# Local attention in a decoder: the second product with the values stationary, probabilities divided ahead of their flip, a norm's bias folded into a weight

## The chip, the cores and the metric

The kernel runs on one core of one Trainium2 chip. The metric is the device time of one execution in microseconds, as the median of several runs; lower is better. The core has TensorE (PE, whose loads of the stationary operand are shown apart as PEld), VectorE (DVE), ScalarE (ACT), GpSimd (POOL) and SyncE (SP), which issues the DMAs. [...]

## The reference

One decoder layer on x of shape (2, 512, 128): a Mamba block with a mixture of experts, cross-attention to a context of 32 rows, and a stack of six layers of local attention and FFN, each of the three followed by a LayerNorm without weights. The change lies in the six-layer stack. With `shift_tokens` (the second half of the channels taken from the token before), 16 heads of 64 and windows of 32 tokens, it is, cut:

```python
def local_attention(q, k, v):            # (b, h, n, d), w = 32
    bq, bk, bv = (t.reshape(b, h, nw, w, d) for t in (q, k, v))
    bk2, bv2 = look(bk), look(bv)        # window before, then own window: 64 keys
    sim = jnp.einsum('bhwie,bhwje->bhwij', bq, bk2) * QK_SCALE
    sim = jnp.where(mask, -jnp.finfo(sim.dtype).max, sim)
    attn = jax.nn.softmax(sim, -1)
    return jnp.einsum('bhwij,bhwje->bhwie', attn, bv2).reshape(b, h, n, d)

def attn_layer(x, Wqkv, qs, ksc, Wo):
    q, k, v = heads of x @ Wqkv
    q, k = l2norm(q) * qs, l2norm(k) * ksc      # then rotary, with a scale by position
    return merge(local_attention(q, k, v)) @ Wo

def ffn_layer(x, g, bln, W1, b1, W2, b2):
    xn = (x - mu) / jnp.sqrt(var + 1e-05) * g + bln
    a, gate = jnp.split(xn @ W1 + b1, 2, -1)
    return a * jax.nn.gelu(gate, approximate=False) @ W2 + b2

for i in range(6):
    x = attn_layer(shift_tokens(x), ...) + x
    x = ffn_layer(shift_tokens(x), ...) + x
```

All arithmetic of the stack is in f32.

## The kernel before

**The front** (Mamba, experts, cross-attention) runs up to about 453 us and is not touched. Then comes the local stack, from line 600 on.

**Layout.** z holds x with channels on partitions, two batches of 512 tokens (plus two columns for the shift). A unit of work is a tile: 128 tokens of one batch in one layer, 6 x 2 x 4 = 48 tiles. Each is an object `Tile` with methods, called at three successive steps of one loop over s: at step s, tile s is A (project, square, rotate, values, sums, norm), tile s-1 is B (flips of q and k, scores, softmax), tile s-2 is C (flip of the probabilities, second product, division, output). An `Ffn` is made when the fourth tile of a batch has been C; it is F1 in the step after (mean, variance, spread) and F2 in the one after that (hidden, out). The loop is inside a block that keeps every engine's queue in program order, so the order of the calls in one step is the order of the queues:

```python
B_.keys_before(); A.begin(); A.project(0); A.square(0); A.rotate(0)
C.flip_p(); F1.mean(); A.project(1); A.square(1); A.rotate(1)
B_.flip_q(); C.attend(); C.weigh(); B_.flip_k(); F2.hidden()
B_.scores(); B_.softmax(); C.flip_o(); B_.expo(); F1.var(); F2.out()
A.values(); A.sums(0); A.sums(1); C.out(); F1.spread(); A.norm(); F1.table()
```

**What each does.** `project` (L712) makes q or k of 128 tokens and 16 heads in a PSUM tile `qk_ps` of 128 x 1024. `square` (L717, ACT) and `rotate` (L724 and L728 on DVE, the sum L733 on POOL) read it. `sums` (L737, DVE) reduces the squares by head. `norm` takes the inverse root: ACT L755, L679 and L680, then POOL L756 and L681 to L684, then POOL multiplies q and k by it (L759, two instructions). `flip_q` and `flip_k` (L892) turn these by eight transposes each, in two groups of four, and ACT copies each group out of PSUM (L893). `scores` puts the mask (L786) and 64 small products (L797) in the PSUM tile `sim`; row 32j + q of it is a query of one window and one head, its columns are four head groups, two slots and 64 keys. `softmax` (L808, L810, DVE) subtracts the row's maximum, `expo` (L814, ACT) takes the exponential.

`flip_p` turns the exponentials (eight transposes of s, L892) into pT, with keys on partitions. `attend` (L833) multiplies: 64 products, each a block of pT (64 keys x 32 queries) as the stationary operand and 65 columns of values as the moving one, of which the last is one, so that column 64 of the result is the sum of the probabilities. The values lie in va (own windows) and vb (shifted by 32 rows, by a DMA from va), both filled with ones at the start (L664). The result, in two PSUM tiles `av`, has queries on partitions. `weigh` (L847, L848, DVE) divides by column 64; `flip_o` (L863) turns the result by eight transposes, which ACT copies to oT (L865, L867); `out` (L882), for two tiles at once and so in every second step, multiplies with Wo, and DVE adds the residual (L885).

**PSUM.** Tag a has three buffers of two banks, for qk_ps (twice a step), av (twice), sim and v_ps. Tag b has two buffers of one bank, for all else.

**FFN.** `mean` subtracts the mean and squares; `var` makes the inverse root; `spread` (L938, DVE) multiplies by it and by ln_g, and POOL adds ln_b (L939); `hidden` multiplies with W1 in three chunks for each half, Gelu on ACT with b1 as bias (L953), and DVE adds b1 of the other half and multiplies (L954); `out` (L963, L966) is the second product.

## Time and profile before

| | |
|---|---|
| time, median of 3 runs | 1481.08 us (1478.0 to 1482.82) |
| the profiled execution's own time | 1485.97 us |
| its span | 1484.2 us |
| PE, DVE, ACT, POOL busy | 1237.8, 908.5, 631.0, 699.6 us |
| granted TensorE clock, mean | 0.912 |
| local stack, first projection to the end | 454.9 to 1484.2 us |
| waits of POOL L756 for ACT L755 (norm) | 294.8 us |
| waits of DVE L724 for ACT L717 | 126.0 us |
| waits of PE's transposes for POOL L759 | 50.9 us |
| waits of POOL L939 for DVE L938 | 27.6 us |

The page gives the busy time of each engine over the whole span, the chain of work that ended last, and the costliest groups of instructions with the idle time ahead of them and what ended it. PE records are pipelined: a matmul's record is longer than its share of the array's time, so distances from start to start say more than durations. Stretches of one step each (from the first qk_ps of a step to that of the next) show what differs between the steps.

### The profile page before, as it was taken

What the parts mean: (1) busy time and instruction counts of PE and PEld (TensorE: products, weight loads), DVE (VectorE), ACT (ScalarE), POOL (GpSimd) and SP (SyncE); (2) the same over time, 40 slices, a digit from 0 to 9 for tenths busy, and PEclk for the clock granted to TensorE, in tenths of its full rate; (3) what the DMA queues carried; (4) which work ended last, traced back from release to release, by engine and by line L of the source; (5) the groups of instructions that cost most, each with busy time, mean ns of one, the idle gap of its engine ahead of it and who ended that gap; (6) DMA issues with size and microseconds to landing.
All of it is one profiled execution on the core that took longest, in us unless ns stands there. A gap on an engine that the chain in (4) does not pass through costs nothing.

```text
span 1484.2 us, 37129 instructions
## 1 busy us (share of the span) xinstructions
PE 1237.8 (83%) x16523; PEld 755.4 (51%) x16523; DVE 908.5 (61%) x1085; ACT 631.0 (43%) x1044; POOL 699.6 (47%) x705
## 2 busy tenths in 40 slices
PE   6686899989646888888898899989888989898865
PEld 2223355545323555655566565656565655555553
DVE  3687866665445665656666565766575666556522
ACT  3333332222113545555555455555555555445521
POOL 1468773100206664564645554647456554455410
PEclk9668999999857999999999999999999999999966
DMA  8122220000300110211121112111021110001000
GB/s 287 59 64 83 78 66 0 30 1 1 131 18 15 42 35 17 70 45 45 31 62 54 30 31 68 47 41 34 17 70 45 42 31 27 27 16 31 27 2 14
DMA packets 39691, 68.04 MB, mean 46 GB/s; under 512 B 4878, under 2 KB 20748, under 8 KB 39532
## 3 DMA queue, kind: packets, MB, share of 16 engines
q1 hardware_dynamic: 39532, 65.68, 14.7%
q8 instruction: 130, 2.13, 0.6%
q14 instruction: 29, 0.24, 0.0%
HBM read 41.00 MB, written 0.70 MB: 28 GB/s over the span
## 4 chain that ended last, share of the span: by engine, by line
PE 52%; DVE 16%; POOL 9%; issue 7%; ACT 7%; POOLq 0%; ACTq 0%; DVEq 0%
PE t_ps L892 6%; PE sim L797 5%; PE wo_ps L882 5%; PE d_ps L403 4%; POOL t L759 4%; PE qk_ps L712 4%; PE av L833 3%; PE v_ps L745 3%; PE g_ps L416 3%; PE u_ps L417 3%; PE fa_ps L951 2%; DVE t L728 2%; PE fg_ps L949 2%; PE fo_ps L963 2%; PE t_ps L863 2%
## 5 line engine op out<-in xcount | busy, mean ns | idle before, releaser
L733 POOL TENSOR_TENSOR t<-t,t 128x1024 f32<-128x1024 f32 x96 | 225.2, 2359 | 30.9 <-DVE rd L847 26.1
L724 DVE TENSOR_TENSOR t<-qk_ps,tab 128x1024 f32<-128x1024 f32 x96 | 117.4, 1223 | 126.0 <-ACT sq L717 126.0
L712 PE MATMUL qk_ps<-wqkv,z 128*128 128x512 f32 x384 | 182.5, 599 | 1.8 <-POOL z L659 1.6
L759 POOL TENSOR_TENSOR t<-t,rn 128x1024 f32<-128x1024 f32 x96 | 180.6, 1903 | 3.8
L892 PE MATMUL t_ps<-ident,t 128*128 128x128 f32 x768 | 115.5, 299 | 51.2 <-POOL t L759 50.9
L756 POOL TENSOR_SCALAR ss<-ss 128x32 f32<-128x32 f32 x48 | 13.7, 286 | 295.8 <-ACT sc L755 294.8
L892 PEld LDWEIGHTS t_ps<-ident,t 128*128 128x128 f32 x768 | 93.9, 153 | 89.6 <-POOL t L759 72.1
L717 ACT ACTIVATE sq<-qk_ps 128x1024 f32<-128x1024 f32 x96 | 98.1, 1023 | 77.8 <-PE qk_ps L712 67.2
L728 DVE TENSOR_TENSOR t<-qk_ps,tab 128x1024 f32<-128x1024 f32 x96 | 116.5, 1213 | 0.0
L737 DVE TENSOR_REDUCE ss<-sq 128x16 f32<-128x1024 f32 x96 | 112.2, 1209 | 0.3
L808 DVE TENSOR_REDUCE m<-sim 128x16 f32<-128x1024 f32 x48 | 58.8, 1224 | 76.4 <-PE sim L797 76.4
L712 PEld LDWEIGHTS qk_ps<-wqkv,z 128*128 128x128 f32 x384 | 70.3, 193 | 64.7 <-issue 60.6
L745 PE MATMUL v_ps<-wqkv,z 128*128 128x512 f32 x192 | 98.8, 640 | 0.0
L278 ACT ACTIVATE da<-dl,acol 128x512 f32<-128x512 f32 x64 | 44.2, 691 | 126.4 <-DVE hs L307 90.1
L295 PE MATMUL y<-hs,ident 128*128 128x512 f32 x128 | 78.3, 746 | 20.2 <-POOL hs L313 12.1
L285 POOL TENSOR_TENSOR db<-dx,b_sb 128x1024 f32<-128x1024 f32 x32 | 76.3, 2390 | 39.5 <-DVE dx L257 22.8
L797 PE MATMUL sim<-kT,qT 64*32 64x64 f32 x6144 | 78.1, 229 | 18.7 <-issue 18.5
L797 PEld LDWEIGHTS sim<-kT,qT 64*32 64x32 f32 x6144 | 66.6, 107 | 43.0 <-issue 41.7
L882 PE MATMUL wo_ps<-oT,wo 128*128 128x256 f32 x384 | 88.2, 383 | 0.0
L893 ACT COPY kT<-t_ps 128x512 f32<-128x512 f32 x96 | 52.6, 588 | 76.0 <-PE t_ps L892 75.8
L882 PEld LDWEIGHTS wo_ps<-oT,wo 128*128 128x128 f32 x384 | 73.8, 193 | 20.3 <-issue 10.8
L833 PE MATMUL av<-va,pT 64*32 64x65 f32 x3072 | 80.9, 248 | 3.5 <-issue 3.2
(232 smaller groups left out, 2411.8 us busy)
## 6 DMA issues: line engine op xcount, KB each, us to landing
vb<-va SPq DMA_DIRECT2D x48, 390.0 KB, 3.6
wqkv<-in_L_ffn_Wqkv_dram SPq DMA_DIRECT2D x18, 512.0 KB, 5.9
b_sb<-bcd SPq DMA_DIRECT2D x32, 256.0 KB, 3.2
c_sb<-bcd SPq DMA_DIRECT2D x21, 256.0 KB, 3.1
vb<-va SPq DMA_DIRECT2D x36, 130.0 KB, 3.4
wo<-in_L_ffn_Wo_dram SPq DMA_DIRECT2D x6, 512.0 KB, 4.3
wg<-in_L_attn_Wg_dram SPq DMA_DIRECT2D x8, 256.0 KB, 6.1
wu<-in_L_attn_Wu_dram SPq DMA_DIRECT2D x8, 256.0 KB, 5.5
```

The lines of the kernel that those rows point to most:

```text
L712: mm(pa[:, hf * S : (hf + 1) * S], self.xb, w[:, w0 : w0 + S], start=True, stop=True)
L717: nc.scalar.activation(sq.rearrange("p h d -> p (h d)"), self.raw[qk], AF.Square)
L724: nc.vector.tensor_mul(t1, pa.rearrange("p (h d) -> p h d", d=DH), tab[:, 2 * qk, ti, :].unsqueeze(1).to_broadcast([P, H, DH]),)
L728: nc.vector.tensor_mul(t2.rearrange("p h (x d) -> p h x d", x=2), swap_halves(pa), tab[:, 2 * qk + 1, ti, :].rearrange("p (x d) -> p x d", ...
L733: nc.gpsimd.tensor_add(t1, t1, t2)
L737: nc.vector.tensor_reduce(self.ss[:, qk], self.sq[qk], AX.X, ALU.add)
L745: mm(pv[:, hf * S : (hf + 1) * S], self.xb, w[:, w0 : w0 + S], start=True, stop=True)
L759: nc.gpsimd.tensor_mul(self.rot[qk], self.rot[qk], self.rn[:, qk].unsqueeze(2).to_broadcast([P, H, DH]),)
L797: mm(ps[32 * j : 32 * j + 32, par, hg, slot, :], qT[64 * r : 64 * r + 64, 2 * hg + c, WIN * w : WIN * (w + 1)], kT[64 * r : 64 * r + 64, 2 ...
L833: mm(po[hh][32 * at : 32 * at + 32, g, i * DV : (i + 1) * DV], pT[rows, 4 * par + hg, 32 * j : 32 * j + 32], (self.v if par else self.v2)[ ...
L882: mm(po, wo_l[:, c, :], self.oT[:, c, :], start=c == 0, stop=c == INNER // P - 1)
L892: tr(pt[:, n, :], src[:, (4 * g + n) * P : (4 * g + n + 1) * P], ident)
```

## The change

Three edits, all in the local stack.

1. **Division ahead of the flip.** `weigh` now belongs to B, after the sums of A: DVE reduces the exponentials over the 64 keys and takes the reciprocal, and POOL multiplies the exponentials by it, in place. The column of ones goes; va and vb have 64 columns, and only the first 32 rows of vb are set to zero at the start.
2. **Values stationary.** `attend` takes 64 columns of values as the stationary operand and 32 columns of pT as the moving one. The result, one PSUM tile, has the channels on partitions and queries along the row, as `out` needs it: two ACT copies (one for each slot) go straight to oT. `flip_o` is gone.
3. **Bias through W1.** `fold_bias` multiplies ln_b with W1 once for each layer, by six one-column products, and DVE adds b1; `hidden` takes this as its bias, and POOL's add in `spread` goes. It is called at the start of the step in which A is tile 2 of batch 0.

```diff
-    va = [big.tile([P, H, DV], F32, name=f"va{j}") for j in range(4)]
-    vb = [big.tile([P, H, DV], F32, name=f"vb{j}") for j in range(3)]
-    for v in va + vb:
-        nc.gpsimd.memset(v, 1.0)
+    va = [big.tile([P, H, DH], F32, name=f"va{j}") for j in range(4)]
+    vb = [big.tile([P, H, DH], F32, name=f"vb{j}") for j in range(3)]
+    for v in vb:
+        nc.gpsimd.memset(v[0:WIN], 0.0)
...
+        def weigh(self):
+            s = self.sf.rearrange("p (x k) -> p x k", k=64)
+            rd = tmp.tile([P, 16], F32, tag="rd", name="rd")
+            nc.vector.tensor_reduce(rd, s, AX.X, ALU.add)
+            nc.vector.reciprocal(rd, rd)
+            nc.gpsimd.tensor_mul(s, s, rd.unsqueeze(2).to_broadcast([P, 16, 64]))
...
         def attend(self):
-            po = [psa.tile([P, 2, S], F32, tag="a", name=f"av{hh}") for hh in range(2)]
-            for g in range(2):
-                for c in range(2):
-                    for r in range(2):
-                        for hh in range(2):
-                            for w in range(4):
-                                slot, par = divmod(w, 2)
-                                hg, j, i = 2 * hh + g, 2 * c + (r ^ par), 2 * c + r
-                                rows, at = slice(64 * slot, 64 * slot + 64), (w + 2 * hh) % 4
-                                mm(
-                                    po[hh][32 * at : 32 * at + 32, g, i * DV : (i + 1) * DV],
-                                    pT[rows, 4 * par + hg, 32 * j : 32 * j + 32],
-                                    (self.v if par else self.v2)[rows, 4 * hg + i, :],
-                                    start=True, stop=True,
-                                )
+            po = psa.tile([P, 2, H // 2, 2, WIN], F32, tag="a", name="av")
+            for hg in range(4):
+                for c in range(2):
+                    for par in range(2):
+                        for slot in range(2):
+                            for r in range(2):
+                                j, i = 2 * c + (r ^ par), 2 * c + r
+                                rows = slice(64 * slot, 64 * slot + 64)
+                                mm(
+                                    po[64 * r : 64 * r + 64, slot, 2 * hg + c, par, :],
+                                    (self.v if par else self.v2)[rows, 4 * hg + i, :],
+                                    pT[rows, 4 * par + hg, 32 * j : 32 * j + 32],
+                                    start=True, stop=True,
+                                )
+            for slot in range(2):
+                t0 = (self.ti % 2) * P + 64 * slot
+                nc.scalar.copy(
+                    self.oT[:, :, t0 : t0 + 64], po[:, slot].rearrange("p c a q -> p c (a q)")
+                )
...
+    def fold_bias(layer, i):
+        w1, pf = layer[2], psb.tile([P, 6], F32, tag="b", name="b1_ps")
+        b1 = lw.tile([P, 6], F32, tag="b1", name=f"b1_{i}")
+        for k in range(6):
+            g, (f0, fs) = k // 3, FCH[k % 3]
+            w0 = g * DFF + f0
+            mm(pf[0:fs, k : k + 1], w1[:, w0 : w0 + fs], col(C_LNB + i), start=True, stop=True)
+            nc.vector.tensor_add(b1[0:fs, k : k + 1], pf[0:fs, k : k + 1], col(C_B1 + 6 * i + k, fs))
+        layer.append(b1)
...
             nc.vector.scalar_tensor_tensor(xc, xc, col(C_LNG + i), spread(self.rs), ALU.mult, ALU.mult)
-            nc.gpsimd.tensor_scalar_add(xc, xc, col(C_LNB + i))
...
+                if (b, ti) == (0, 2):
+                    fold_bias(layers[i], i)
...
             if C:
                 C.attend()
-                C.weigh()
...
                 B_.softmax()
-            if C:
-                C.flip_o()
             if B_:
                 B_.expo()
...
                 A.sums(0)
                 A.sums(1)
+            if B_:
+                B_.weigh()
             if C:
                 C.out()
```

More of the change, by code (lines that the diff above doesn't have):

```diff
@@ L627, in load_layer @@
         tab = lw.tile([P, 4, 4, DH], F32, tag="tab", name=f"tab_{i}")
-        return wqkv, wo, w1, w2, tab, qs
+        return [wqkv, wo, w1, w2, tab, qs]
     def scale_tables(layer):
-        tab, qs = layer[4:]
+        tab, qs = layer[4:6]
         nc.gpsimd.tensor_mul(tab, rot, qs.unsqueeze(2).to_broadcast([P, 4, 4, DH]))
@@ L649, in decoder_kernel @@
     NTB = S // P
-    DV = DH + 1
     z = big.tile([P, B, S + 2], F32, name="z")
@@ L746, in values @@
             v = self.v = va[n % 4]
-            nc.scalar.copy(v[:, :, 0:DH], pv.rearrange("p (h d) -> p h d", d=DH))
+            nc.scalar.copy(v.rearrange("p h d -> p (h d)"), pv)
             v2 = self.v2 = vb[n % 3]
@@ L820, in attend @@
         def attend(self):
-            pT = self.pT
-            po = [psa.tile([P, 2, S], F32, tag="a", name=f"av{hh}") for hh in range(2)]
-            for g in range(2):
-                for c in range(2):
-                    for r in range(2):
-                        for hh in range(2):
-                            for w in range(4):
-                                slot, par = divmod(w, 2)
-                                hg, j, i = 2 * hh + g, 2 * c + (r ^ par), 2 * c + r
-                                rows, at = slice(64 * slot, 64 * slot + 64), (w + 2 * hh) % 4
-                                mm(
-                                    po[hh][32 * at : 32 * at + 32, g, i * DV : (i + 1) * DV],
-                                    pT[rows, 4 * par + hg, 32 * j : 32 * j + 32],
-                                    (self.v if par else self.v2)[rows, 4 * hg + i, :],
-                                    start=True, stop=True,
-                                )
-            self.po = po
-        def weigh(self):
-            po = self.po
-            o = self.o = tmp.tile([P, H, DH], F32, tag="o", name="o", bufs=1)
-            for hh in range(2):
-                pe = po[hh][:, :, 0 : 4 * DV].rearrange("p g (i e) -> p g i e", e=DV)
-                rd = tmp.tile([P, 2, 4], F32, tag="rd", name="rd")
-                nc.vector.reciprocal(rd, pe[:, :, :, DH])
-                nc.vector.tensor_mul(
-                    o[:, 8 * hh : 8 * hh + 8, :].rearrange("p (g i) d -> p g i d", g=2),
-                    pe[:, :, :, 0:DH], rd.unsqueeze(3).to_broadcast([P, 2, 4, DH]),
-                )
-        def flip_o(self):
             if self.ti % 2:
@@ L857, in flip_o @@
                 self.oT = tmp.tile([P, H // 2, 2 * P], F32, tag="oT", name="oT")
-            dst = self.oT[:, :, (self.ti % 2) * P : (self.ti % 2 + 1) * P]
-            of = self.o.rearrange("p h d -> p (h d)")
-            for g in range(2):
-                pt = psb.tile([P, 4, P], F32, tag="b", name="t_ps")
-                for n in range(4):
-                    tr(pt[:, n, :], of[:, (4 * g + n) * P : (4 * g + n + 1) * P], ident)
-                if g == 0:
-                    nc.scalar.copy(dst[:, 0:4, :], pt)
-                else:
-                    nc.scalar.copy(
-                        dst[:, 4:8, :].rearrange("p c (x t) -> p c x t", x=2),
-                        bass.AP(
-                            tensor=pt.tensor, offset=pt.offset + 64,
-                            ap=[list(pt.ap[0]), [P, 4], [-64, 2], [1, 64]],
-                        ),
-                    )
+            pT = self.pT
+            po = psa.tile([P, 2, H // 2, 2, WIN], F32, tag="a", name="av")
[17 more added lines that the diff above has]
+                )
         def out(self):
@@ L921, in spread @@
         return sd
+    def fold_bias(layer, i):
[7 more added lines that the diff above has]
+        layer.append(b1)
     class Ffn:
         def __init__(self, i, b, layer):
-            self.i, self.b, (self.w1, self.w2) = i, b, layer[2:4]
+            self.i, self.b, (self.w1, self.w2), self.b1 = i, b, layer[2:4], layer[6]
         def mean(self):
@@ L952, in hidden @@
                 ge = ftmp.tile([P, S], F32, tag="ge", name="ge", bufs=2)
-                nc.scalar.activation(ge[0:fs], pg[0:fs], AF.Gelu, bias=col(C_B1 + 6 * i + 3 + c, fs))
+                nc.scalar.activation(ge[0:fs], pg[0:fs], AF.Gelu, bias=self.b1[0:fs, 3 + c : 4 + c])
                 nc.vector.scalar_tensor_tensor(
-                    hid[0:fs, c, :], pa[0:fs], col(C_B1 + 6 * i + c, fs), ge[0:fs], ALU.add, ALU.mult
+                    hid[0:fs, c, :], pa[0:fs], self.b1[0:fs, c : c + 1], ge[0:fs], ALU.add, ALU.mult
                 )
```

## The prediction

> **What bounds the kernel now.** I read the page first: engines, then the chain of work that ended last.

> ```profile
> PE 1237.8 (83%) x16523; PEld 755.4 (51%) x16523; DVE 908.5 (61%) x1085; ACT 631.0 (43%) x1044; POOL 699.6 (47%) x705
> PE 52%; DVE 16%; POOL 9%; issue 7%; ACT 7%; POOLq 0%; ACTq 0%; DVEq 0%
> ```

> TensorE is busy for 83% but holds only 52% of the chain: it is not the only limit. The change lies in the local stack, 48 steps from 454.9 us (first qk_ps of step 0) on. The step repeats in rounds of four, told apart by what C and the FFN add: R1 (C is tile 2: nothing), R2 (tile 3: wo_ps), R3 (tile 0, and F1), R4 (tile 1: wo_ps, and F2). Second, the busy times of four stretches, one round (layer 3, first batch), cut where each step's first qk_ps starts:

> ```profile
> 922.89:935.91 13.02, 12.74 (x303) 8.69 (x302) 9.66 (x13) 6.16 (x11) 9.81 (x9) 1.00 0.34 107
> 935.91:955.21 19.30, 17.21 (x320) 12.45 (x319) 13.21 (x14) 11.73 (x20) 10.35 (x12) 0.91 0.12 36
> 955.21:974.08 18.87, 16.08 (x322) 10.72 (x321) 12.45 (x15) 10.36 (x20) 10.45 (x13) 1.00 0.19 54
> 974.08:1001.27 27.19, 24.99 (x338) 14.25 (x337) 15.70 (x18) 13.52 (x20) 11.85 (x12) 1.00 0.18 51
> ```

> The columns are stretch, length, busy us of PE, PEld, DVE, ACT, POOL, the clock, DMA. R1 is all PE; R2 to R4 have 2 to 3 us each in which PE waits. For what, the timeline of each engine tells. In R2, on POOL and then PE:

> ```profile
> 938.55 0.28 POOL L756 TENSOR_SCALAR ss<-ss 128x32 f32<-128x32 f32 x1 [5.23 <-ACT sc L755]
> ...
> 940.52 3.76 POOL L759 TENSOR_TENSOR t<-t,rn 128x1024 f32<-128x1024 f32 x2
> ```
> ```profile
> 935.91 1.88 PE L712 MATMUL qk_ps<-wqkv,z 128*128 128x512 f32 x4
> 937.63 1.04 PE L892 MATMUL t_ps<-ident,s 128*128 128x128 f32 x8
> 938.50 1.88 PE L712 MATMUL qk_ps<-wqkv,z 128*128 128x512 f32 x4
> ```

> PE has done both projections by 940.4 and then waits to 942.5 for the norm's first product. This loop bounds R2: flip_q, scores, softmax, sums (both on DVE), norm (ACT, then POOL), flip_q. The sums end at 938.10, 4.77 us after the scores end; the first L759 ends 4.32 later. In R4 the same wait is 1.86 us, there because the bias stands in POOL's queue ahead of the norm:

> ```profile
> 975.13 1.58 POOL L939 TENSOR_SCALAR ln_xc<-ln_xc,cols 128x512 f32<-128x512 f32 x1 [2.10 <-DVE ln_xc L938]
> 976.78 0.29 POOL L756 TENSOR_SCALAR ss<-ss 128x32 f32<-128x32 f32 x1
> ...
> 978.45 3.77 POOL L759 TENSOR_TENSOR t<-t,rn 128x1024 f32<-128x1024 f32 x2
> ```

> In R3 PE waits 1.28 us at ln_sd for the variance's chain through softmax, exponential, ACT and POOL.

> [...] eight 128-column loads of ln_var take 0.97 us, 111 ns from one to the next. [...] the 128 records of L833 (64 products, two records each) take 1.49 us, their loads 1.33, some 10 ns each[...]. [...] after R2's wait L833 took 2.07 us at clock 0.50, with no wait 1.49:

> ```profile
> 943.50:945.70 2.20, 2.07 (x128) 1.83 (x128) 0.50 0.04 7
> 962.30:963.90 1.60, 1.49 (x128) 1.33 (x128) 1.00 0.00 0
> ```

> [...] Here 1.90 us (L759) against 1.22 (L810).

> **Part by part, each step.**
> *Removed from PE:* the eight transposes of o, 0.87 us (eight at 109 ns).
> *attend:* still 64 products, 128 records, but stationary 64x64 (values) instead of 64x32, moving 32 columns instead of 65, on four places of the array instead of eight. No row shows this shape. Now a block holds PE for 1.42 us at best (128 at 10.0 ns and 0.15 until the next). [...] I take 1.85, since full-array transposes[...] come every 109 ns, so a load hides a product. [...] So +0.43 -0.87 = -0.44 us of PE a step.
> *DVE:* two reciprocals and two products go (1.78 us); a reduce (1.21, as L737) and a reciprocal (0.20) come, after the sums. They hide under PE work; what matters is what follows them.
> *POOL:* a product of 128x1024 by a broadcast factor, 1.90 (L759's form), queued **ahead of the norm**. It waits for reduce and reciprocal, so it ends at sums + 3.45. Queued behind it: the norm's five small operations (1.74 from a predecessor's end to L759, as at 976.71 to 978.45) and its two products. First product out at sums + 7.1 instead of + 4.3. And flip_p of the next step, which stands ahead of the second projection on PE, now waits for sums + 3.5; before, it waited for nothing.
> *ACT:* as many copies, but the two of oT (1.07) now stand ahead of kT's; scores start about 0.4 later than kT allowed before.
> *PSUM:* five tiles of tag a a step instead of six, in three buffers: scores no longer wait for the second rotate but for the first. Gains 0.1 to 0.3 in R1 and R3.
> *Bias:* L939 goes, 12 times 1.58 plus its wait.
> *fold_bias:* six times twelve records of 111 ns (1.3 us) and six small DVE adds, at the start of R3 of batch 0. PE waits there at flip_p anyway (below); without that cover, 8 us in all. I take 3.

> Times from a step's first qk_ps, qk_ps 1.73 each, flips 0.87, value projection 1.72, wo_ps 3.45, scores 1.4 after kT's first copy:
> - R1: sums at -1.1 (as now), so flip_p 2.4 (arrives 1.73), flip_q 6.0 (arrives 5.0), attend to 8.7, kT copied from 9.74, scores to 11.8, values to **13.5** (now 13.0). Sums at 16.6, 3.1 into R2.
> - R2: flip_p waits from 1.73 to 6.6, second projection to 9.2, flip_q at 10.2, attend to 12.9, scores to 16.0, values and wo_ps to **21.2** (now 19.3). Sums at 20.8, -0.4 in R3.
> - R3: flip_p 3.1, flip_q 6.75, scores to 12.55, as now; ln_sd by the unchanged chain at 18.0: **19.0** (18.9). The transposes saved are swallowed by that wait. Sums 17.3; the weighing ends 20.8, the first L759 at 24.4, now 25.1: the bias was dearer than the weighing.
> - R4: flip_q 5.45 (now 6.3), attend to 8.2, hidden from 9.75 (now 10.1) for 5.96, scores to 17.7, fo_ps straight behind (now 19.3), values and wo_ps to **25.6** (27.2).

> Sum 79.3 against 78.4: +0.9 a round, twelve rounds: +11. The clock: R2's new idle time halves it too, but while there is slack ahead of flip_q; I put 0.3 each on R2 and R4. Before, R4 lost 0.8 on the mean (28.1 in ten full rounds, 27.2 undisturbed), and R2's loss is in its 19.3. Balance -0.2, times 12: -2. Many blocks of L833 already have holes in their issue (1.78 us on the mean over 48); slower records hide part: -2. fold_bias +3. Tail, last two tiles without company: reduce, reciprocal, weighing (3.4) against the old weighing and flip (3.0), and 1.6 for the bias: about -1 to -2. Sum +8. The start gains 0.3 at most (the memsets ran beside the first projection).

> The profiled execution took 1485.97 us (span 1484.2, 1.8 around it), 4.9 above the median 1481.08 of three runs. So 1494 by its own measure; against the median I forecast **1489**.

> **Rivals.**
> *A, faster: [...]* If 64-column loads hide fully, attend stays 1.42: 48 x 0.43 = 21 us less, 1468. For it: the first 32 records of a block start every 7 ns. [...] The sum turns at about 12 ns a record (1.68 a block); below that, the saved transposes and the 1.7 us of R4 outweigh R2.
> *B, load and product in turn on each place:* [...] 1525. [...] Against it: the transposes at 109 ns.
> *C, the change doesn't do what it says:* the four places don't overlap across columns; [...] 1565. [...]

> **Chances.** Forecast case 0.45 (its own range 1478 to 1500, from the fetch holes, the clock, the cover of fold_bias), A 0.33, B 0.17, C 0.05. Within 0.3% (4.4 us) is about what a measurement can't tell from no change. Of the forecast case 0.24 is slower, 0.15 the same, 0.06 faster; of A 0.27 faster, 0.06 the same; B and C slower. So faster 0.33, same 0.21, slower 0.46. The range leaves C and a part of B and A out: 1466 to 1525.

> **What would show it.** The spacing of the value products: 13 ns a record, block 1.85. R2 near 21 us with PE idle 4 to 5 us ahead of the transposes of s, released by POOL's new product; R4 near 25.6 with its wait for L759 under 1 us; R3 unchanged, ended by ln_sd; POOL busy +70 us (48 x 1.9 less 19). I am wrong if a block takes 1.5 us or 2.5, or if PE doesn't wait at the transposes of s.

## The result, and the profile after

The changed kernel takes **1580.12 us** (median of 4, 1575.84 to 1582.38) against 1481.95 before (4 runs): ratio 1.0665, 95% interval 1.0637 to 1.0694. It is slower by 98 us. The forecast had the sign, but not the size: 1489, in a range up to 1525. The profiled execution took 1582.38 us (span 1580.6).

The page of the changed kernel, engines and chain:

```profile
PE 1269.4 (80%) x16211; PEld 765.0 (48%) x16211; DVE 899.7 (57%) x1025; ACT 629.6 (40%) x1044; POOL 767.9 (49%) x737
PE 49%; DVE 22%; ACT 7%; POOL 7%; issue 6%; POOLq 0%; DVEq 0%; ACTq 0%
```

PE has 312 records fewer and yet is busy 32 us longer. In the chain PE lost three points and DVE won six, three of them by the division's reduce (L819). The page's groups of instructions show the new wait (line, engine, operation, tiles, count | busy us, mean ns | idle us before it and who ended it):

```profile
L821 POOL TENSOR_TENSOR s<-s,rd 128x1024 f32<-128x1024 f32 x48 | 91.3, 1901 | 353.5 <-DVE rd L820 347.7
L872 PE MATMUL t_ps<-ident,s 128*128 128x128 f32 x384 | 65.3, 325 | 76.1 <-POOL s L821 76.1
L872 PE MATMUL t_ps<-ident,t 128*128 128x128 f32 x768 | 109.1, 287 | 20.6 <-POOL t L758 20.3
```

The transposes of s wait 76.1 us for POOL's product; those of q and k wait 20.6, where it was 51.2. The mean ns are of records that overlap: a flip's eight transposes take 0.87 us at full clock from its start to the next instruction's (937.63 to 938.50 before). One round of four steps (layer 5, first batch), cut at each step's first qk_ps, columns as in the prediction:

```profile
1322.69:1336.89 14.20, 12.56 (x295) 8.06 (x294) 7.45 (x10) 6.25 (x10) 11.90 (x11) 1.00 0.03 8
1336.89:1364.03 27.14, 19.44 (x323) 13.98 (x322) 16.74 (x22) 11.79 (x20) 15.00 (x17) 0.93 0.14 41
1364.03:1385.00 20.97, 17.30 (x314) 11.45 (x314) 11.54 (x12) 10.71 (x20) 10.19 (x11) 0.91 0.04 9
1385.00:1411.02 26.02, 25.32 (x330) 14.55 (x330) 15.09 (x15) 12.73 (x20) 11.36 (x11) 0.95 0.09 28
```

R4 is near its forecast (25.6), R1 and R3 are 0.7 and 2.0 us over theirs (13.5 and 19.0), and R2 is 6 us over its 21.2. PE in that R2:

```profile
1336.89 1.88 PE L711 MATMUL qk_ps<-wqkv,z 128*128 128x512 f32 x4
1343.52 1.97 PE L872 MATMUL t_ps<-ident,s 128*128 128x128 f32 x8 [4.75 <-POOL s L821]
1345.29 2.49 PE L711 MATMUL qk_ps<-wqkv,z 128*128 128x512 f32 x4
1347.62 1.04 PE L872 MATMUL t_ps<-ident,t 128*128 128x128 f32 x8
...
1355.81 3.62 PE L862 MATMUL wo_ps<-oT,wo 128*128 128x256 f32 x16
1359.26 0.28 PE L910 MATMUL b_ps<-cols,w 128*128 128x1 f32 x2
1361.27 0.38 PE L910 MATMUL b_ps<-cols,w 128*128 128x1 f32 x2 [1.73 <-DVE b L911]
1361.90 0.31 PE L910 MATMUL b_ps<-cols,w 128*85 128x1 f32 x2 [0.25 <-DVE b L911]
...
1363.73 0.44 PE L910 MATMUL b_ps<-cols,w 128*85 128x1 f32 x2 [0.25 <-DVE b L911]
```

Two things cost here. The flip of s begins 6.63 us into the step, as forecast to a tenth, after a wait of 4.75; but then its eight transposes take 1.77 us (1343.52 to 1345.29) instead of 0.87 and the second projection 2.33 (to 1347.62) instead of 1.73; the granted clock was 0.50 over the transposes and 0.74 over the projection. And fold_bias, from 1359.26 to the next step's 1364.03, holds PE 4.77 us. DVE in those microseconds tells why:

```profile
1358.82 1.21 DVE L819 TENSOR_REDUCE rd<-s 128x16 f32<-128x1024 f32 x1
1360.07 0.25 DVE L820 RECIPROCAL rd<-rd 128x16 f32<-128x16 f32 x1
1360.23 0.79 DVE L865 TENSOR_TENSOR za<-z,wo_ps 64x256 f32<-64x256 f32 x2
1361.06 0.16 DVE L911 TENSOR_TENSOR b<-b_ps,cols 128x1 f32<-128x1 f32 x1
1361.69 0.16 DVE L911 TENSOR_TENSOR b<-b_ps,cols 128x1 f32<-128x1 f32 x1 [0.47 <-PE b_ps L910]
```

The first add is queued on DVE behind the division's reduce and the sums of za, so it comes 1.5 us after its product. From then on product and add take turns, since all six share one PSUM tile and each product waits for the add before it (`<-DVE b L911` above): 0.63 us a pair (1361.06 to 1361.69). The six folds take 8.0, 5.0, 5.3, 5.7, 4.7 and 4.8 us, 33.5 in all.

### The profile page after: what moved, and what is told of

The parts are those of the page before. It is cut to its first block, busy times and chain, and to the rows that moved or that the text cites. A ratio compares the mean times of both kernels' runs of the same rounds, so it can differ in the third digit from the quotient of the medians.

```text
span 1580.6 us, 36499 instructions
## 1 busy us (share of the span) xinstructions
PE 1269.4 (80%) x16211; PEld 765.0 (48%) x16211; DVE 899.7 (57%) x1025; ACT 629.6 (40%) x1044; POOL 767.9 (49%) x737
## 4 chain that ended last, share of the span: by engine, by line
PE 49%; DVE 22%; ACT 7%; POOL 7%; issue 6%; POOLq 0%; DVEq 0%; ACTq 0%
PE qk_ps L711 7%; PE av L843 6%; PE t_ps L872 6%; DVE ss L736 6%; PE sim L796 5%; PE d_ps L403 4%; ACT oT L851 3%; DVE rd L819 3%; PE g_ps L416 3%; DVE m L807 3%; DVE s L809 3%; PE u_ps L417 2%; PE fa_ps L941 2%; PE fg_ps L939 2%; POOL t L758 2%
## 5 line engine op out<-in xcount | busy, mean ns | idle before, releaser
L821 POOL TENSOR_TENSOR s<-s,rd 128x1024 f32<-128x1024 f32 x48 | 91.3, 1901 | 353.5 <-DVE rd L820 347.7
L711 PE MATMUL qk_ps<-wqkv,z 128*128 128x512 f32 x384 | 214.7, 689 | 1.8 <-POOL z L658 1.6
L758 POOL TENSOR_TENSOR t<-t,rn 128x1024 f32<-128x1024 f32 x96 | 180.6, 1903 | 3.8
L813 ACT ACTIVATE s<-s 128x1024 f32<-128x1024 f32 x48 | 50.7, 1057 | 200.2 <-DVE s L809 200.2
L872 PE MATMUL t_ps<-ident,s 128*128 128x128 f32 x384 | 65.3, 325 | 76.1 <-POOL s L821 76.1
L872 PE MATMUL t_ps<-ident,t 128*128 128x128 f32 x768 | 109.1, 287 | 20.6 <-POOL t L758 20.3
L711 PEld LDWEIGHTS qk_ps<-wqkv,z 128*128 128x128 f32 x384 | 81.0, 225 | 75.9 <-issue 72.0
L872 PEld LDWEIGHTS t_ps<-ident,t 128*128 128x128 f32 x768 | 89.9, 147 | 57.7 <-POOL t L758 40.7
L872 PEld LDWEIGHTS t_ps<-ident,s 128*128 128x128 f32 x384 | 54.1, 169 | 115.0 <-POOL s L821 104.0
L843 PE MATMUL av<-pT,va 64*64 64x32 f32 x3072 | 96.5, 222 | 3.5 <-issue 3.2
L843 PE MATMUL av<-pT,vb 64*64 64x32 f32 x3072 | 96.8, 223 | 0.0
L796 PE MATMUL sim<-kT,qT 64*32 64x64 f32 x6144 | 75.3, 228 | 21.2 <-issue 13.9
```

The source lines that it names most:

```text
L711: mm(pa[:, hf * S : (hf + 1) * S], self.xb, w[:, w0 : w0 + S], start=True, stop=True)
L758: nc.gpsimd.tensor_mul(self.rot[qk], self.rot[qk], self.rn[:, qk].unsqueeze(2).to_broadcast([P, H, DH]),)
L796: mm(ps[32 * j : 32 * j + 32, par, hg, slot, :], qT[64 * r : 64 * r + 64, 2 * hg + c, WIN * w : WIN * (w + 1)], kT[64 * r : 64 * r + 64, 2 ...
L843: mm(po[64 * r : 64 * r + 64, slot, 2 * hg + c, par, :], (self.v if par else self.v2)[rows, 4 * hg + i, :], pT[rows, 4 * par + hg, 32 * j ...
L872: tr(pt[:, n, :], src[:, (4 * g + n) * P : (4 * g + n + 1) * P], ident)
```

## The experiments

Two theories came out of this. **F**: the fold's issue in series costs some 30 us. **W**: the rest is the early division, put ahead of the flip of s and of the norm. Their rivals: the new product itself, and the halved clock behind the new waits. Below, "half clock" is the time that the records show at clock 0.5 between the first step's start and the last one's: 82 us before, 150 after. A microsecond at clock 0.5 is taken to cost about half a microsecond at most. This is an estimate from three pairs, at half clock and at full: 1.77 and 0.87 us for the flip of s just shown, 2.07 and 1.49 for the old value product in the prediction, 3.64 and 2.02 for the records of the new one (e3 and the change, below). PE waits are the idle times ahead of the transposes of s, of those of q and k, and of ln_sd, over the span. Means of a step R1 to R4 leave out the first round, in which parts of the work are still missing. For each run: median, and ratio to the kernel before with its 95% interval.

**e1, the fold in two loops** (1549.46; 1.0463, 1.0427 to 1.0498):

```
         for k in range(6):
...
             mm(pf[0:fs, k : k + 1], ...)
-            nc.vector.tensor_add(b1[0:fs, k : k + 1], ...)
+        for k in range(6):
+            fs = FCH[k % 3][1]
+            nc.vector.tensor_add(b1[0:fs, k : k + 1], ...)
```

> The changed kernel with one edit: fold_bias issues its six products first and then its six adds. Theory F (the fold runs in series: in the changed kernel each product waits for the add of the one before, 4.7 to 8.0 us a fold, 33.5 us in all, and the projection behind it runs at half clock): the fold falls to some 1.5 us, the time to about 1548 us. Theory W (what was not foreseen lies at the wait of the flip of the probabilities for the weighing, and in the clock that this wait halves): TensorE waits there anyway in the next step, so the fold is mostly covered, and the time stays above 1568 us.

31 us less than the change. The products' row, of the change and then of e1:

```profile
L910 PE MATMUL b_ps<-cols,w 128*128 128x1 f32 (+1 forms) x72 | 15.0, 278 | 19.3 <-DVE b L911 19.3
```
```profile
L910 PE MATMUL b_ps<-cols,w 128*128 128x1 f32 (+1 forms) x72 | 7.5, 231 | 0.0
```

The wait of 19.3 us is gone and the products take half as long. F holds. All that follows but e2, e8 and e11 has the fold in two loops.

**e2, the change without its third edit** (1569.07; 1.0616, 1.0575 to 1.0657): no fold_bias, and POOL's bias in `spread` again.

> The changed kernel without its third edit: no fold_bias, the bias is added by GpSimd in spread as before. Theory F: some 42 us less for the fold and its clock, some 18 us more since the add stands behind the weighing and ahead of the norm in twelve steps: about 1556 us. Theory W: the fold was covered, the add is not: 1590 us.

Between the two forecasts. Against e1 the bias on POOL is dear (+20): R4 is 27.68 us on the mean against 25.89, its wait at the flip of q 1.42 against 0.25, since the bias stands in POOL's queue ahead of the norm again. So the third edit is worth 20 us with its adds behind its products; as written it loses those 20 and 11 more.

**e3, e1 without the division** (1484.48; 1.0029, 1.0010 to 1.0048): `B_.weigh()` left out.

> The kernel of e1_fold_loops with weigh left out altogether, so the output is not divided by the sums of the probabilities: the price of reduce, reciprocal and product with all that waits for them. Theory W: the waits at the flip of the probabilities (4.5 us in the second step of a round, 0.5 in the others) go, and with them the half clock behind them: about 60 us less than e1_fold_loops, some 1488 us. Theory F alone: what is left after the fold is a slower second product, so no more than 25 us less, some 1525 us.

65 us less than e1. The row of the flip of s, of e1 and then of e3:

```profile
L872 PE MATMUL t_ps<-ident,s 128*128 128x128 f32 x384 | 63.1, 317 | 81.7 <-POOL s L821 81.3
```
```profile
L872 PE MATMUL t_ps<-ident,s 128*128 128x128 f32 x384 | 51.8, 278 | 4.7 <-ACT s L813 3.8 <-DVE za L865 0.6
```

PE waits fall from 137.3 us to 74.0 in all, about as much as the time does. W holds for the waits. Its second half doesn't: half clock was to go too, and it rises from 106 to 140 us. And nothing is won against the kernel before, although e3 has no division and no flip of o.

**e5, the third edit alone, fold in two loops, on the kernel before** (1456.30; 0.9841, 0.9804 to 0.9878).

> The kernel before with the third edit alone, its fold issued as in e1_fold_loops (six products, then six adds). Theory F: GpSimd's add goes from ahead of the norm, so the wait of 1.9 us in the fourth step of each round goes, and each fold costs some 1.5 us: 8 to 15 us less than before, some 1468 us. Theory W2 (the third edit gives nothing, the clock or another wait takes it back): within 4 us of before.

More than expected, 23 us, and the fastest kernel of all here that computes the whole reference. R4 falls from 28.06 to 25.38 on the mean: with the bias gone from POOL, flip_q there no longer waits, where it waited 1.86 us, and half clock falls from 82 to 41 us over the whole stack.

**e11, the third edit alone, fold in series** (1486.64; 1.0040, 1.0018 to 1.0062): e5 with the adds back in the first loop.

> The kernel before with the folded bias alone, each product followed by its add as in the change. Theory 'the order in series costs 31 us wherever it stands': 1456 + 31 = 1487, no gain left of the third edit. Rival 'the fold hides in the kernel before, where PE has other slack': 1456 to 1465.

30 us above e5, as 31 in the change. The issue in series has the same price in both kernels and eats the third edit's gain whole.

**e9, e5 with the early division, the old product kept** (1533.00; 1.0372, 1.0349 to 1.0395):

```
+            if B_:
+                B_.divide()          # reduce, reciprocal, POOL product
...
-                nc.vector.tensor_mul(o..., pe[:, :, :, 0:DH], rd...)
+                nc.vector.tensor_copy(o..., pe[:, :, :, 0:DH])
```

> The kernel before with the folded bias (six products, then six adds) and the early division alone: reduce, reciprocal and POOL's product after the sums, the old value product and the flip of o kept, the row of ones unused, av copied by two plain copies on DVE. Theory 'the division's price is its place and does not depend on the product': 1456 + 65 = 1515 to 1525, R2 waits 4.4 us at the flip of s. Rival 'the division is dear only together with the new product': 1465 to 1490.

77 us above e5, 8 over the range given, and somewhat more than its 65 in the new product's company: the division's price doesn't depend on the new product. That its place alone makes the price is not shown by this. PE waits rise from 52.9 to 110.4 us; the one at the flip of s in R2 is 3.4 us, where 4.4 was forecast. R1 is 2.06, R2 2.88, R4 0.95 us longer on the mean, the tail 7.5. And the new product on top (e1) costs 16 more, where the forecast had it gain 21.

**e13, e3 with eight useless transposes where the flip of o stood** (1490.37; 1.0073, 1.0051 to 1.0094), and **e14, e5 without the transposes of o** (1438.17; 0.9696, 0.9653 to 0.9740): oT is copied from o as it stands, so ACT reads SBUF there and doesn't wait for PE.

> The kernel without the division (its output lacks it) with eight useless transposes of pT in the place where the flip of o stood. Theory 'PE time saved there is swallowed by waits that come later and halve the clock': the time stays within 1470 to 1492 (1484 without the transposes), half clock in R2 falls from 7.7 to under 5 us, waits at the flip of q and at ln_sd shrink by about 1 us. Rival 'the transposes were on the path and something of the new product itself costs the 28 us': 1484 + 42 = 1526.

> The kernel before with the folded bias (products, then adds) and the old product, the eight transposes of o left out: oT is copied from o as it stands, so that the output lacks the flip. Theory 'swallowed': 1445 to 1465 (1456 with them), the wait at the flip of q in R2 or at ln_sd in R3 longer, half clock up. Rival 'on the path': 48 x 0.87 = 42 us less, 1414 to 1425; then the swallowing belongs to the new product's own dependencies.

48 times 0.87 us of transposes, 42 us of PE, are worth 6 in the new kernel and 18 in the old. The rows of e3, then e13:

```profile
L872 PE MATMUL t_ps<-ident,t 128*128 128x128 f32 x768 | 116.8, 302 | 35.9 <-POOL t L758 35.9
...
L900 PE MATMUL ln_sd<-ident,ln_rs 128*128 128x128 f32 x112 | 23.0, 370 | 33.4 <-POOL ln_rs L683 33.4
```
```profile
L878 PE MATMUL t_ps<-ident,t 128*128 128x128 f32 x768 | 112.7, 294 | 29.8 <-POOL t L758 29.6
...
L906 PE MATMUL ln_sd<-ident,ln_rs 128*128 128x128 f32 x112 | 21.3, 350 | 20.7 <-POOL ln_rs L683 20.7
```

With the useless work PE waits 18.8 us less in these two places, and half clock falls from 140 to 96 us, worth up to half of the 44. So PE's saved time turns into waits for the norms that POOL computes, and with these waits comes the halved clock. In the old kernel, e5 and then e14:

```profile
L892 PE MATMUL t_ps<-ident,t 128*128 128x128 f32 x768 | 108.6, 286 | 31.0 <-POOL t L759 29.6 <-issue 1.4
...
L920 PE MATMUL ln_sd<-ident,ln_rs 128*128 128x128 f32 x112 | 19.6, 329 | 18.6 <-POOL ln_rs L684 18.6
```
```profile
L881 PE MATMUL t_ps<-ident,t 128*128 128x128 f32 x768 | 110.4, 290 | 38.2 <-POOL t L759 36.6 <-issue 1.6
...
L909 PE MATMUL ln_sd<-ident,ln_rs 128*128 128x128 f32 x112 | 23.8, 378 | 32.5 <-POOL ln_rs L684 32.5
```

21.1 of the 42 us came back as waits there too. The step from e14 to e3 (new product, no flip in either, no division in e3) costs 46. The block of 128 records of the value product takes 1.72 us on the mean of all 48 in e14 and 2.50 in e3, which is 37 of the 46. At full clock it is some 0.5 us longer (medians 1.59 and 2.07). At half clock the new product loses far more: the six blocks of e14 that lie wholly in it have a median of 2.07 us, the eleven of e3 3.64. One of them:

```profile
1264.80:1268.60 3.80, 3.64 (x128) 3.51 (x128) 0.00 (x0) 0.50 0.02 4
```

Half clock rises from 73 to 140 us in all. The two alternatives were too sharp: e14 lies between them, and both the swallowing and the product's own cost are real.

**e4, e1 with five useless products ahead of the flip of s in R2** (1544.35; 1.0426, 1.0379 to 1.0473), **e7, e3 with two ahead of its flip of q** (1478.53; 0.9993, 0.9966 to 1.0021), **e8, the kernel before with the same two** (1494.99; 1.0100, 1.0065 to 1.0136):

```
+    def warm(w, n):
+        d = psb.tile([P, S], F32, tag="b", name="warm_ps")
+        for k in range(n):
+            mm(d, ones_inv, w[:, k * S : (k + 1) * S], start=True, stop=True)
...
+                if C.ti == NTB - 1:
+                    warm(C.layer[0], n)
```

> The kernel of e1_fold_loops with five products of no use (4.3 us) on TensorE ahead of the flip of the probabilities in the second step of each round, where it waits 4.5 us anyway. They take away the idle time, not the wait. Theory W with the clock (2.2 us at half clock in that step before, 6.5 after): 17 to 29 us less than e1_fold_loops. If the clock costs nothing because flip_q waits for the norm in any case: within 5 us of it.

> The kernel of e3_no_division (no division, so the output lacks it), with two products of no use (1.7 us) on TensorE ahead of flip_q in the second step of each round, where it waits 2.3 us. Theory H (the clock: in e3_no_division that wait is followed by 10 us at half clock, 7.7 us in the mean second step against 2.2 before[...]): 25 to 35 us less than e3_no_division, some 1455 us. If the clock is not the cause: within 5 us of it.

> The kernel before with the same two products of no use ahead of flip_q in the second step of each round, where it waits 1.8 us in the mean. Theory H: only some 1.7 us of half clock a round can go there[...]: 5 to 12 us less than before. If the old kernel suffers as much from the clock as the new one: 25 us less.

The theories with the clock missed all three times; in e4 and e7 the small rival forecast (within 5 us) is about what came. The useless products do keep the clock up: half clock falls from 106 to 75 us in e4, from 140 to 81 in e7, from 82 to 51 in e8. The time doesn't follow: 5 and 6 us less, with intervals that overlap those of e1 and e3, and in e8 15 more, the cause of which is not settled. In e4, R2 goes only from 24.11 to 23.47, although 4.2 us of half clock go from it: PE, on time again, now waits 0.72 us at the flip of q for the norm behind the division, which accounts for part of it. In e7 the products stand where PE waited 2.29 us, half clock in R2 falls from 7.7 to 1.3, and R2 is only 1.43 us shorter: PE now stands idle 1.26 us ahead of the scores instead of 0.18. So keeping the clock up was by itself worth little in these kernels.

**e6, e1 with the division's product on DVE, and the flip of s behind the second projection** (1593.48; 1.0769, 1.0725 to 1.0813), **e10, e6 with three useless products ahead of that flip** (1577.06; 1.0665, 1.0641 to 1.0690), and **e12, e1 with the flip moved alone** (1634.36; 1.1036, 1.0981 to 1.1092):

```
-            if C:
-                C.flip_p()
...
                 A.rotate(1)
+            if C:
+                C.flip_p()
             if B_:
                 B_.flip_q()
```

> The kernel of e1_fold_loops, with the product of weigh on VectorE instead of GpSimd, and flip_p called after the second projection instead of ahead of it. Theory W (place and engine of the weighing make its price: it stands ahead of the norm on GpSimd, and the flip that waits for it stands ahead of the second projection): the norm is no later than before and the flip waits behind work that is due anyway, so the time comes near to e3_no_division, 1485 to 1500 us. If the price is the added work itself, wherever it is: 1530 us or more.

> The kernel with the division's product on DVE and the flip of s after the first rotate, with three useless products of 512 columns ahead of that flip in the steps behind a wo_ps. Theory 'that kernel lost by the halved clock, 13 us of it in R2': half clock in R2 falls to under 4 us and R2 from 25.5 to 23 or less, R3 by 1 to 2 us, time 1535 to 1560. Rival 'the DVE that is busier holds the rest': R2 stays at 25 or above, time 1585 or more.

> The changed kernel with the fold as six products and then six adds, and the flip of s moved from ahead of the second projection to behind it, the division left on POOL. Theory 'the wait at the flip is one of order, PE could project meanwhile': the wait at the flip in R2 falls from 4.5 to 2.5 or less, time 1500 to 1525 against 1549. Rival 'what waits is the whole chain of division and norm behind the sums': the wait moves to the flip of q, time 1540 to 1560.

In e10 the flip stands where e6 has it, behind the second projection and its rotates, not behind the first rotate, and the useless products stand in R2 alone. These three were to make the division cheaper, and missed by the most. e12 differs from e1 by the place of one flip and is 85 us slower. It differs from e6 only by the engine of the product, and e6 is 41 us faster: so it is the moved flip that costs, and DVE was the cheaper engine beside it. The product on DVE with the flip left in its old place was not tried.

The R2 of e12 as a stretch, and PE in it:

```profile
1284.06:1310.87 26.81, 21.21 (x311) 15.06 (x310) 15.04 (x15) 11.91 (x20) 12.80 (x12) 0.75 0.09 26
```
```profile
1284.06 3.60 PE L711 MATMUL qk_ps<-wqkv,z 128*128 128x512 f32 x8
1290.69 1.09 PE L872 MATMUL t_ps<-ident,s 128*128 128x128 f32 x8 [3.04 <-POOL s L821]
1294.35 1.97 PE L872 MATMUL t_ps<-ident,t 128*128 128x128 f32 x8 [2.56 <-POOL t L758]
```

The flip of s starts at 6.63 us, when it did in e1. The projection now lies ahead of the wait, so behind it only eight transposes are left to do before PE waits again, 2.56 us, for the norm. The three waits make 170 us over the span (137 in e1), 22.9 of them new: the flips of s and q now stand next to each other and share two PSUM buffers, so q's waits for ACT's copies of pT. Worse, half clock rises from 106 to 290 us, which by the estimate above can cost up to 92: the mean clock of this R2 is 0.75. In e1 the second projection follows the long wait. e10 brings e6's 256 us of half clock down to 161 and R2 from 25.50 to 22.68, but R3, where no products were put, stays at 23.4 (half clock 5.9 us of it), and the run ends at 1577, between the two forecasts and nearer the rival.

Laid end to end, by the medians: before 1480, third edit with the fold in two loops -24 (e5), early division +77 (e9), values stationary without the flip of o +16 (e1), fold in series +31 (the change): 1580. The split depends on the order: laid the other way, the new product is +28 (e3 against e5) and the division +65 (e1 against e3).

## Why the prediction was wrong, step by step

- **attend:** right in kind, somewhat short in size. A block in the change at full clock, 128 records:

```profile
1348.50:1350.60 2.10, 2.02 (x128) 1.96 (x128) 0.00 (x0) 1.00 0.03 8
```

 2.00 us to the next instruction (1348.58 to 1350.58), so 14.5 ns a record with the 0.15 us behind the last one taken off, where 1.85 us and 13 ns were forecast. The difference makes 7 us in 48 steps. Rival A (1.42 us) falls, and so do B and C, since the block stays well under the 2.5 us that the forecast set as its upper mark. For full-array transposes the kernel before shows the overlap that the forecast went by: eight, each with a load and a product, come 109 ns apart, eight loads of ln_var alone 111, and a projection's products take 108 for 128 columns (1.73 us for four of 512). How far loads and products overlap in the new shape was the author's estimate, in the rivals too. What the forecast left out is the product at half clock, 3.64 us a block in e3.
- **Transposes of o removed:** the step that failed most. The forecast booked them in R1, R2 and R4 (in R3 it saw them swallowed) and, with the longer product, netted 0.44 us a step, 21 us. With the division out of the way (e3 against e5) the new product and the missing flip together are 28 slower: 49 us off. By e14, 24 of these are transposes that gave nothing (worth 18 of 42), gone into waits at flip_q and ln_sd; the other 25 are the product (46 where 21 was forecast), about half of it by estimate in blocks at half clock: they add 0.35 us to the mean block of e3 and 0.08 to that of e14, 13 us in 48. R1, where PE hardly waits, bears the forecast out: undisturbed it is 12.34 us in e3 and 12.7 in the kernel before, 0.4 less.
- **fold_bias:** forecast at 3 us, under the cover of a wait, from "twelve records of 111 ns" a fold and six small adds. It costs 31 (e1), 30 (e11). The code puts a DVE add between two products on one PSUM tile; I counted the instructions and overlooked their order. In the change the first add also queues behind the division's reduce on DVE and the folds are longer for it, but e11, without that reduce, pays the same. The cover itself was right. In e1 one fold takes 1.11 us, and in the two rounds shown, one with a fold and one without, the flip of s starts 6.63 us after the first wo_ps of R2 (1324.17 and 895.26):

```profile
1327.62 1.25 PE L910 MATMUL b_ps<-cols,w 128*128 128x1 f32 x12
1330.80 1.09 PE L872 MATMUL t_ps<-ident,s 128*128 128x128 f32 x8
```
```profile
901.89 1.09 PE L872 MATMUL t_ps<-ident,s 128*128 128x128 f32 x8 [1.30 <-POOL s L821]
```

 The wait of 1.30 us can cover 1.1 us, but not 4.7 to 8.0: in the change the flip of s behind a fold starts 11.2 to 12.7 us after that wo_ps.
- **The division (DVE, POOL, flip_p):** its chain was right. POOL's product takes 1.90 us, POOL is busy 68 us more (forecast 70), the flip of s waits 4.5 us on the mean of R2 (4.9 forecast) and 0.65 in R1 (0.7), and R1's flip_q starts at 6.1 us (forecast 6.0). What came after it in R2 was forecast too short: e1's R2, without the 0.51 us that its folds take on the mean, is 23.6 against 21.2.
- **The clock:** "while there is slack ahead of flip_q; I put 0.3". In R2 of e1 the flip of s takes 1.61 us on the mean instead of 0.87 and the two projections 4.86 instead of 3.62: 2.0 us, not 0.3, and that is the size of most of R2's error. e4 qualifies this: with the clock kept up, R2 wins only 0.6 of it.
- **R3** should have been unchanged. It is 20.52 on the mean (19.00 before), 19.88 in e1. A fold in series ahead of it leaves its first projection at half clock (3.26 us at 1364.03, granted clock 0.55, where 1.73 is usual). It does end with ln_sd, as said: in the round shown 19.5 us after the step's start, 1.5 of them from the slow projection, where 18.0 was forecast. The wait at ln_sd is 2.68 us instead of 1.09. That is not the fold's doing: it is 2.68 in e1 as well, 2.47 in e3 and 2.38 in e14, but 1.18 in e9, which has the flip of o, and 1.31 in e13, where useless transposes stand in its place. So it goes with the missing transposes.
- **R4** right: 26.17 on the mean, 26.02 in the round shown, forecast 25.6; the wait at L758 is 0.34 (forecast under 1). But e5 shows that the bias alone gives more than that (25.38).
- **Tail:** forecast 1 to 2 us shorter. From the last step's start it is 112.3 us, before 104.8; the division makes 5.7 of it (e1 110.3, e3 104.6).

In sum, from the first step's start to the last one's the change took 1016.1 us in its profiled execution and the kernel before 924.4: 92 more, where the forecast had some 10. That is 82 of the 91 us by which the forecast fell short; the tail is the rest. By the runs, 28 of the 91 lie with the fold (31 less the 3 forecast), 49 with the new product and the lost transposes, and the remaining 14, by subtraction, with the division and the bias. How much of the last two is the clock isn't settled to the microsecond: waits and half clock feed each other, which is what e4, e7 and e13 show.

## What to carry to other kernels

Price PE time saved only up to the next wait on another engine: put the saving into the step's timetable, see what PE waits for next, and treat what lies behind that wait as lost. Price an operation's new shape at half clock too, if it stands behind a wait: here the block of the value product got 0.5 us longer at full clock and 1.6 at half. Small products into one PSUM tile that another engine reads between them ran at the round trip's pace, 0.63 us a pair, so issue all products first and then the reads. An operation put ahead of two users in one queue delayed both: with the division's product ahead of the norm and of the flip of s, PE waits were 137.3 us (e1), without it 74.0 (e3). Moving one user later doesn't help if that takes away the work that PE did between two waits (e12, 85 us slower than e1).

## What the runs showed of the hardware

**The value product's shape.** 64 f32 products in 128 records, at full clock: 1.42 us to the next instruction at best with 32 columns stationary and 65 moving, 2.00 with 64 stationary and 32 moving. Wholly at half clock the records of a block took 2.07 us (shown in the prediction) and 3.64 us (e3): the first shape loses 0.6 us against its 1.49 at full clock, the second 1.6 against its 2.07.

**VectorE and POOL.** The division's product of 128x1024 takes 1.90 us on POOL (the change) and 1.22 on DVE (e6). In e6, where it ran on DVE with both operands in SBUF, a POOL operation on 128x32 that started with it took 1.33 us, about as long as the product's 1.22:

```profile
1168.24 0.25 DVE L820 RECIPROCAL rd<-rd 128x16 f32<-128x16 f32 x1
1168.53 1.22 DVE L821 TENSOR_TENSOR s<-s,rd 128x1024 f32<-128x1024 f32 x1
```
```profile
1168.20 0.25 POOL L680 TENSOR_TENSOR na<-ss,rn 128x32 f32<-128x32 f32 x1 [0.39 <-ACT rn L679]
1168.53 1.33 POOL L681 TENSOR_TENSOR na<-na,rn 128x32 f32<-128x32 f32 x1
```

L681 takes 0.25 us in the change, and over 1 us at 44 places in e6. So the norm stood still for about 1.1 us in most steps of e6, and that limits what the product gains on DVE. What makes the one wait for the other was not shown.
